# Means on 32-column tiles, a moved copy, and earlier zeroes in a four-layer graph network on one core

## The chip, the cores and the metric

The kernel runs on one core of a Trainium2 chip. The metric is the device time of one execution in microseconds (us), smaller is better. The core has five engines that work side by side and wait for each other by semaphores: TensorE (PE in the profile, its weight loads PEld), VectorE (DVE), ScalarE (ACT), GpSimd (POOL) and SyncE (SP). Transfers are issued from the queues of SP, ACT and POOL and share 16 DMA engines.

## The reference, cut to what matters

Four graph layers stand one behind the other, each as `x = x + layer(relu(layernorm(x)))`, on `x` of 8 batches, 2048 nodes, 64 features, all float32. The change touches layers 0 and 1 and the layer norm at the entrance of layer 2.

```python
def _layernorm(x):                       # over the 64 features
    m = mean(x); v = var(x)
    return (x - m) / sqrt(v + 1e-5)

def layer0(x, H, adj, W, W_ind, a_node, a_gn, a_ge, fcW, fcb, av):
    h = x @ W                                            # [8, 2048, 64]
    s = leaky_relu(h @ a_node, 0.2)
    alpha = softmax(where(H.T > 0, s, NEG))              # over the nodes of each of 64 hyperedges
    agg = einsum('ben,bnf->bef', alpha, h)
    beta = sigmoid((h @ a_gn)[:, None, :] + (agg @ a_ge)[:, :, None])
    all_he = elu(beta[..., None] * h[:, None] + (1 - beta[..., None]) * agg[:, :, None])
    deg = maximum(adj.sum(-1), 1.0)[:, None]
    industry = einsum('nm,bmf->bnf', adj / deg, x @ W_ind)
    attn = lambda f: tanh(f @ fcW + fcb) @ av
    coefs1 = softmax(where(H > 0, attn(elu(agg)), NEG))  # over the edges of each node
    g = einsum('bne,benf->bnf', coefs1, all_he)
    pair = stack([industry, g]); return sum(softmax(attn(pair)) * pair)

def layer1(x, adj, W, a):
    h = x @ W
    e = leaky_relu((h @ a[:64])[:, :, None] + (h @ a[64:])[:, None, :], 0.2)
    att = softmax(where(adj > 0.5, e, NEG_INF), axis=2)
    return elu(att @ h)

def layer2(x, adj, ...):   # three rounds of  v = relu([v, adj @ v] @ W1.T + b1) @ W2.T + b2
def layer3(x, adj, ...):   # x, adj @ x and (2 adj adj - 1) @ x, each through weights of the node's own
```

## The kernel before, in words

Two batches of 64 features fill the 128 partitions, so there are NP = 4 pairs p, each a 128 x 2048 matrix; CW = 512 columns are a chunk, NCW = 4 chunks make a pair, NT = 16 blocks of 128 nodes make 2048. The program goes through stages, which the trace shows one behind the other.

*Stage N* (to about 46 us) normalizes x and makes the first chunk of `industry`. *Stage E* (about 46 to 225 us) walks over the other three chunks in `industry(c)`: for each of eight loads `at` of the adjacency it issues 16 wide matmuls `acc` (L1098) and adds the load into the degree sum `ds`. Between them it pops small pieces of other work from the list `units`: `members(i)` (one for each block of nodes; it writes the high part `hi` and the rest `lo` of its features, stores both in DRAM, and adds to the sums `pg`, `pd` of the hyperedges), `listing` (which slots a node's edges take: `ranks`, `numbers`), and `table_1` to `table_5` (the tables by hyperedge). `hi` and `lo` come from a pool of three buffers each; their last 8 columns are set to zero by `begin()` (L1156) before each use. `table_5` makes 18 products `pn`, each of 8 columns. Stage E is not written in strict order: a scheduler at build time orders each engine's instructions, by priority and its own estimate of when operands come, and hands out buffers as they come free. An instruction issued through `InOrder` (or by `mm` and `turn` while `kit.strict` is set) stays behind everything that the source has issued before on its engine.

*Stage L* (about 225 to 375 us) goes over LT = 18 tiles of 114 nodes, NB = 3 blocks of slots in each: step j is block k = j % 3 of tile i = j // 3. TensorE's order is strict here. `features(i)` loads the `hi` and `lo` rows of a tile (`hhi`, `hlo`, three buffers each, 235 KB a load, POOL's queue), at step k = 2 for tile i + 2. `shares(i+1)`, also at k = 2, is the first reader of these (products `pm`). The slots of the first tile, `sT0` and `tmp0`, take one buffer of `hlo` and one of `hhi`. In the same steps the stage loads twelve 1 MB tiles `aT` of the adjacency (POOL's queue, `load_early`), and copies three pairs of x from DRAM to DRAM, 1 MB each (`x1_dram[i // 4]`, shown as `xd<-in_xT`). These copies are written at tiles 4, 8 and 12 and issued through `S = InOrder(nc.sync)`. `divided`, `back`, `done` scale a finished tile, turn it, and write it away.

*Stage O* (about 375 to 440 us) mixes `industry` and g, and `first_neighbours` makes layer 1's features of pair 0 in between.

*Stage A* (about 440 to 838 us) is layer 1's attention, four pairs in two halves of 16 blocks m. For each block, DVE makes two tiles `pt` (128 x 1024, L1793, six buffers), and TensorE multiplies them on tiles of 32 columns: `o` (features, weights `hS`) and `dn` (sums, weights `vd`). Between blocks, `between(m)` lets the next pair's preparation advance by `n` steps:

```python
n = (m in LATE) + 2 * (m == 2 * NT - 1) if last else (2, 0, 1, 0, 1)[m % 5] - (m % 20 == 0)
```

The preparation is `neighbour_steps(p + 1)`; per chunk it has a mean (`kit.norm_steps`: one matmul of 512 columns with the 128 x 128 matrix `avg` as weights), a variance (the same once more), and two steps `ph` with two maps each (weights of 128 columns, 132 columns moving). At the last pair it is `Layers23.front`, with four means and four variances by `norm_steps` at the blocks in LATE. The rows R that DVE needs (512 KB each, from `r_dram`) are loaded by SP's queue. For the last pair the pool `near` (R, and `l1_sb` with raw, sc, vd, wd, rstd, varn, rs, hS, xc, x, q, rr in this order) is closed, and two R buffers of a new pool `l1_late` take memory that partly was `l1_sb`'s. Pairs 0 and 2 have their `hS` in `l1_sb`, pairs 1 and 3 in `att_sb`.

*Layers 2 and 3* follow to the end.

Of the kernel before, what the change touches and what calls it, by code (L numbers as in the profile page):

```python
# [8 lines left out]
FP = mybir.dt.float32  # L9
# [7 lines left out]
P = 128  # L17
# [14 lines left out]
def cols(c, w=CW):  # L32
    return slice(c * w, (c + 1) * w)
# [603 lines left out]
class Kit:  # L637
# [110 lines left out]
    def use_ln_exp(self):  # L748
        self.tc.keep_in_program_order(self.nc.scalar.preload_act_table_set(LN_EXP))

    def norm_steps(self, dst, src, mean, var, xc, q):

        nc, mm = self.nc, self.mm
        n = dst.shape[-1] // CW
        for c in range(n):
            mm(mean[:, cols(c)], self.avg, src[:, cols(c)], start=True, stop=True)
        nc.vector.tensor_sub(xc, src, mean)
        nc.scalar.activation(q, xc, AF.Square)
        yield
        for c in range(n):  # L760
            if callable(var):
                var = var()
            mm(var[:, cols(c)], self.avg, q[:, cols(c)], start=True, stop=True)
        nc.scalar.activation(q, var, AF.Ln, bias=self.eps)
        nc.scalar.activation(q, q, AF.Exp, scale=-0.5)
        nc.vector.scalar_tensor_tensor(dst, xc, 0.0, q, op0=OP.max, op1=OP.mult)
        yield
# [6 lines left out]
def layer0(kit, hn, x1_dram, open_early, late_tile, between):  # L774
# [40 lines left out]
    def features(i):  # L815

        hi = lst.tile([P, B * F + 2 * B], FR, tag="hhi", name="hhi", bufs=3)
        lo = lst.tile([P, B * F + 2 * B], FR, tag="hlo", name="hlo", bufs=3)
        nc.gpsimd.dma_start(out=hi[0:LN], in_=hi_dram[of(i)].bitcast(FR))
        nc.gpsimd.dma_start(out=lo[0:LN], in_=lo_dram[of(i)].bitcast(FR))  # L820
        return hi, lo
# [16 lines left out]
    with ExitStack() as sA:  # L838
# [234 lines left out]
        with ExitStack() as s1:  # L1073
# [4 lines left out]
            pd = ps.tile([P, B], FP, tag="pd", name="pd")  # L1078
            units = []

            def industry(c, own):
# [62 lines left out]
            def members(i):  # L1144
# [4 lines left out]
                def begin():  # L1149
                    hi = sb.tile([P, BF_ + 2 * B], FR, tag="hi", name="hi", bufs=3)  # L1150
                    lo = sb.tile([P, BF_ + 2 * B], FR, tag="lo", name="lo", bufs=3)
                    es = sb.tile([P, B], FP, tag="es", name="es")
                    hs = sb.tile([P, B, F], FP, tag="hs", name="hs")
                    held.extend((hi, lo, es, hs))
                    for v in (hi, lo):
                        nc.vector.memset(v[:, BF_ + B :].bitcast(FP), 0.0)  # L1156
                    part(0)
# [93 lines left out]

            def table_5():

                pn = ps.tile([P, LT, B], FP, tag="pd", name="pn")
                for i in range(LT):
                    mm(pn[0:LN, i, :], MT[:, of(i)], kept["ea"][0:E, B : 2 * B], start=True, stop=True)
                nc.vector.tensor_scalar_max(rden[0:LN], pn[0:LN], 1e-30)
                nc.vector.reciprocal(rden[0:LN], rden[0:LN])
# [31 lines left out]
            units += rest  # L1290
            units += [last, table_1]
            units += [lambda: None, table_2, lambda: None, table_3, lambda: None, table_4, table_5, first_nodes]
            own = out_of(0, acc, None)
            for c in range(1, NCW):
                own = industry(c, own)
            for unit in own + units:
                unit()
        loaded = [features(i) for i in range(2)]

# [4 lines left out]
    with ExitStack() as s0:  # L1304
# [5 lines left out]

        V, A, G = InOrder(tc, nc.vector), InOrder(tc, nc.scalar), InOrder(tc, nc.gpsimd)
        mm = kit.mm
        flat = lambda a: a.rearrange("p b f -> p (b f)")
# [115 lines left out]
        for j in range(last + 2 * NB):  # L1429
            i, k = divmod(j, NB)  # L1430
            there = i + 1 < LT
            if k == 0:
                if 0 < i < LT:
                    shared(i)
                if 3 < i <= LT:
                    done(i - 4)
            if k == 2 and there:
                turned(i + 1)
            if j < last:
                pairs_of(j)  # L1440
            if k == 1 and i + 2 < LT:
                next_nodes(i + 2)
            if 1 <= j <= last:
                mixed(j - 1)
            if 3 <= j < last + 3:
                weighed(j - 3)
            if 5 <= j < last + 5:
                gathered(j - 5)
            if k == 0 and there:
                ranks(i + 1)  # L1450
            if k == 1 and there:
                turn(i + 1)
                edges(i + 1)
            if k == 2:
                if there:
                    shares(i + 1)
                if i + 2 < LT:
                    loaded.append(features(i + 2))
                if i < LT:
                    load_early(i)  # L1460
                if i in (4, 8, 12):
                    S.dma_start(out=x1_dram[i // 4], in_=t["xT"][i // 4])
                if 2 < i < LT:
                    back(i - 3)
                if 1 < i:
                    divided(i - 2)
                if i >= LT:
                    if i == LT:
                        back(i - 3)
                        done(i - 3)  # L1470
                    back(i - 2)
                    done(i - 2)
# [102 lines left out]
class Layer1:  # L1575
# [22 lines left out]
    def neighbour_steps(self, p):  # L1598
# [11 lines left out]
        for c in range(NCW):  # L1610
# [9 lines left out]
            if hS is None:  # L1620
                hS = (self.sb2 if p % 2 else sb).tile([P, NT, P], FP, tag="hS", name="hS", bufs=1)
            for g in range(2):
                if g:
                    yield
                ms = slice(4 * c + 2 * g, 4 * c + 2 * g + 2)
                ph = ps.tile([P, 2, P + 4], FP, tag="h", name="ph")
                for k in range(2):
                    j = 2 * g + k
                    mm(ph[:, k, :], hn[:, j * P : (j + 1) * P], Wx, start=True, stop=True)
                nc.scalar.activation(vd[:, ms, :], ph[:, :, P : P + 2], AF.Exp, scale=0.2)  # L1630
# [18 lines left out]
    def first_neighbours(self, xs, V, A):  # L1649
# [10 lines left out]
        rs = sb.tile([P, 2, NT], FP, tag="rs", name="rs", bufs=1)  # L1660
        hS = sb.tile([P, NT, P], FP, tag="hS", name="hS", bufs=1)
        mean, xc, q, out = {}, {}, {}, []
# [24 lines left out]

        def mapped():
            for m, ph in out:
                A.activation(hS[:, m : m + 2, :], ph[:, :, 0:P], AF.Copy)  # L1690
                V.tensor_copy(raw[:, m : m + 2, :], ph[:, :, P:])
            out.clear()
# [26 lines left out]
        def scaled(c):  # L1719
            h = hS[:, NC4 * c : NC4 * c + NC4, :].rearrange("p t (b f) -> p t b f", b=2)  # L1720
            V.tensor_tensor(
# [26 lines left out]
        self.first = [self.scores(0, 0, None) for b2 in range(2)]  # L1748
        self.now = hS, vd, wd
        at = lambda f, *a: lambda: f(*a)  # L1750
# [110 lines left out]
    def run(self, aT, following):  # L1861
# [10 lines left out]
        for p in range(NP):  # L1872
# [7 lines left out]
            def between(m):  # L1880
                if m % NT and ends:
                    ends.pop(0)()

                n = (m in LATE) + 2 * (m == 2 * NT - 1) if last else (2, 0, 1, 0, 1)[m % 5] - (m % 20 == 0)
                for _ in range(n):
# [494 lines left out]
```

## Time and profile before

| | us |
|---|---|
| runs of the kernel before | 1913.49 median of 3 (1909.81 to 1913.96) |
| the profiled execution | 1914.77 |
| its span | 1913.0 (mean granted TensorE clock 0.989) |
| TensorE busy | 1860.1 (97%) |
| DVE / ACT / POOL busy | 1176.0 / 464.2 / 314.9 |

The span runs from the first to the last instruction of the program; 1.8 us of the execution's own time lie around it. Instructions are named by engine, line and the tiles that they write and read; `L632` and `L737` are the helpers through which all ordered and all strict instructions go. A float32 matmul shows as two records. In brackets behind a line of the timeline stand the engine's idle time before it and what ended it.

### The profile page before, as it was taken

To read this page: it belongs to the slowest core of one execution; us is meant where nothing else is said; L and a number is where in the kernel's file an instruction comes from. 1 tells how busy PE (TensorE), PEld (TensorE's weight loads), DVE (VectorE), ACT (ScalarE), POOL (GpSimd) and SP (SyncE) were. 2 spreads that over 40 slices of the span, in tenths; PEclk is the share of its full clock that TensorE was granted. 3 is DMA by queue.
4 is the path that set the end of the run, shared out by engine and by line. 5 is a ranking of instruction groups with operands and counts; after the bars stand their busy time and mean duration, and the time that the engine had idled before them with its cause. 6 is when DMAs were issued, how large, how long until landed. Compare 5 with 4: busy or idle time off the path is not lost.

```text
span 1913.0 us, 25771 instructions
## 1 busy us (share of the span) xinstructions
PE 1860.1 (97%) x10172; PEld 1135.7 (59%) x10172; DVE 1176.0 (61%) x1869; ACT 464.2 (24%) x1048; POOL 314.9 (16%) x435
## 2 busy tenths in 40 slices
PE   7999989999999998999999999999999999999997
PEld 7877767543333232257775577765587755677653
DVE  7765579889898988953327642446623276523465
ACT  5422346573222120111210111310112201113000
POOL 4111278411000000000002110112200021101122
PEclk9999989999999999999999999999999999999999
DMA  7665386475222222213101021100122011121000
GB/s 205 169 198 176 126 227 169 108 176 117 57 56 57 56 49 53 62 42 100 61 12 30 26 61 56 50 23 19 33 66 61 23 25 31 45 72 50 5 20 13
DMA packets 86373, 142.60 MB, mean 75 GB/s; under 512 B 33800, under 2 KB 34056, under 8 KB 83568
## 3 DMA queue, kind: packets, MB, share of 16 engines
q1 hardware_dynamic: 65072, 83.78, 15.1%
q0 software_dynamic: 21040, 56.98, 12.3%
q8 instruction: 82, 1.34, 0.3%
q14 instruction: 51, 0.42, 0.1%
q10 hardware_dynamic: 128, 0.07, 0.0%
HBM read 106.85 MB, written 37.09 MB: 75 GB/s over the span
## 4 chain that ended last, share of the span: by engine, by line
PE 72%; issue 15%; DVE 5%; DMA 5%; POOL 2%; ACT 1%; SPq 0%; POOLq 0%; DVEq 0%; ACTq 0%
PE acc L737 32%; PE u L737 14%; PE o L737 5%; PE acc L1098 3%; PE py L737 3%; PE dn L737 3%; PE pgs L737 2%; PE pd L737 2%; DVE pt L1793 1%; PE var L737 1%; PE mean L737 1%; PE pv L737 1%; PE pm L737 1%; DMA hlo<-lo_dram 1%; DMA den<-d_dram 1%
## 5 line engine op out<-in xcount | busy, mean ns | idle before, releaser
L737 PE MATMUL acc<-aT,parts 128*128 128x512 f32 x1664 | 441.4, 409 | 0.0
L737 PEld LDWEIGHTS acc<-aT,parts 128*128 128x128 f32 x1664 | 306.6, 188 | 97.8 <-issue 39.2
L737 PE MATMUL o<-pt,hS 128*32 128x512 f32 x2048 | 237.9, 596 | 6.3 <-DVE pt L1793 5.2
L1793 DVE SCALAR_TENSOR_TENSOR pt<-R,wd,aT 128x1024 f32<-128x1024 f32 x188 | 230.7, 1279 | 21.0 <-DMA R<-r_dram 13.9
L737 PE MATMUL u<-W3f,y 64*128 64x512 f32 x1024 | 241.7, 589 | 0.0
L2255 DVE TENSOR_TENSOR pr<-u,embf 128x512 f32<-128x512 f32 x256 | 170.6, 687 | 109.7 <-PE u L737 102.7
L737 PEld LDWEIGHTS u<-W3f,y 64*128 64x128 f32 x1024 | 100.8, 187 | 119.0 <-issue 119.0
L737 PEld LDWEIGHTS o<-pt,hS 128*32 128x32 f32 x2048 | 64.8, 110 | 161.1 <-issue 144.4
L737 PE MATMUL u<-W3f,v 64*128 64x512 f32 x512 | 133.5, 596 | 0.0
L2267 POOL TENSOR_TENSOR fold<-fold 128x256 f32<-128x256 f32 x64 | 47.7, 745 | 496.1 <-DVE fold L2266 496.1
L737 PE MATMUL dn<-pt,vd 128*32 128x512 f32 x1024 | 125.0, 597 | 0.0
L2046 DVE TENSOR_TENSOR yb<-py,cb_f 128x512 f32<-128x512 f32 x32 | 22.1, 692 | 157.7 <-PE py L737 157.7
L1098 PE MATMUL acc<-at,Y 128*128 128x512 f32 x384 | 105.8, 418 | 0.2 <-ACT ev L1128 0.2
L737 PE MATMUL acc<-aTl,parts 128*128 128x512 f32 x384 | 99.7, 398 | 0.0
L2143 POOL TENSOR_TENSOR bq<-bq,xp 128x512 f32<-128x512 f32 x16 | 20.7, 1291 | 421.6 <-ACT xp L2126 421.6
L2259 DVE TENSOR_TENSOR pr<-pr 128x512 f32<-128x512 f32 x128 | 88.1, 688 | 2.2
L737 PEld LDWEIGHTS u<-W3f,v 64*128 64x128 f32 x512 | 56.6, 186 | 49.8 <-issue 36.5
L1793 DVE SCALAR_TENSOR_TENSOR pt<-R,wd,aTl 128x1024 f32<-128x1024 f32 x64 | 79.2, 1280 | 9.9 <-PE dn L737 6.2
L737 PEld LDWEIGHTS acc<-aTl,parts 128*128 128x128 f32 x384 | 71.5, 188 | 16.2
L1098 PEld LDWEIGHTS acc<-at,Y 128*128 128x128 f32 x384 | 71.4, 195 | 15.6 <-issue 1.8
L737 PEld LDWEIGHTS dn<-pt,vd 128*32 128x32 f32 x1024 | 31.0, 110 | 74.4 <-issue 69.9
L2060 DVE TENSOR_TENSOR parts<-tp,parts 128x512 fp32r<-128x512 f32 x16 | 11.1, 692 | 85.3 <-ACT parts L2059 85.3
(372 smaller groups left out, 2696.3 us busy)
## 6 DMA issues: line engine op xcount, KB each, us to landing
at<-in_adjT POOLq DMA_DIRECT2D x32, 512.0 KB, 5.2
raw<-in_adjT SPq DMA_DIRECT2D x64, 256.0 KB, 3.3
aT<-in_adjT POOLq DMA_DIRECT2D x12, 1024.0 KB, 7.9
xp<-xd SPq DMA_DIRECT2D x45, 256.0 KB, 2.9
R<-r_dram SPq DMA_DIRECT2D x14, 512.0 KB, 3.8
hlo<-lo_dram POOLq DMA_DIRECT2D x18, 235.1 KB, 3.7
hhi<-hi_dram POOLq DMA_DIRECT2D x18, 235.1 KB, 3.4
hi_dram<-hi SPq DMA_DIRECT2D x16, 264.0 KB, 3.2
```

The lines of the kernel that those rows point to most:

```text
L737: one = self.nc.tensor.matmul(*args, **kw)
L1098: mm(acc[p], Y[h][:, m, p, :], at[:, k, :], start=m + h == 0, stop=m == NT - 1 and h == 1)
L1793: V.scalar_tensor_tensor(pt, R, w, a.bitcast(FP), op0=OP.max, op1=OP.mult)
L2046: nc.vector.tensor_tensor(yb, py, bias[:, None, :].to_broadcast([P, 4, P]), op=OP.add)
L2060: nc.vector.tensor_tensor(lo, tp, hi.bitcast(FP), op=OP.subtract)
L2143: nc.gpsimd.tensor_add(bq, bq, xp)
L2255: nc.vector.tensor_tensor(a, u[h], emb[:, i, 8 * w : 8 * w + 8, None].to_broadcast([P, 8, F]), op=OP.mult)
L2259: nc.vector.tensor_add(pr[h], pr[h], a)
L2267: nc.gpsimd.tensor_add(fold[:, :, 0:2, :], fold[:, :, 0:2, :], fold[:, :, 2:4, :])
```

## The change

It has seven parts.

- `norm_steps` no longer multiplies by `avg` as one 128 x 128 tile. The new `averages` issues four matmuls, each with 32 columns of `avg` as weights, writing 32 partitions. `norm_steps` serves layer 1's chunks of pairs 1 to 3 and `front`.
- In `neighbour_steps` the four maps of a chunk are made in one step, into two PSUM tiles (tags `ln` and `h`), and `between` takes one step at m % 5 in (0, 2, 4). The maps keep their 128-column weights.
- In `first_neighbours`, `hS` is allocated at its first use in `mapped`, behind `xc`, `x` and `q`, no longer at the beginning.
- The three copies of x go through ACT's queue, in its program order.
- `members` takes its buffers from three pairs made once, whose zero columns are written once.
- `features(0)` and `features(1)` are issued in POOL's order among the last units of stage E; `table_5` is split into six units of three products, behind `first_nodes`.
- At the end of stage L, `back(14)`, `divided(15)` and `done(14)` move from tile 17 and step 54 to step 56.

```diff
+    def averages(self, dst, src):
+        for q in range(0, P, 32):
+            self.mm(dst[q : q + 32, :], self.avg[:, q : q + 32], src, start=True, stop=True, tile_position=(0, q))
...
-        for c in range(n):
-            mm(mean[:, cols(c)], self.avg, src[:, cols(c)], start=True, stop=True)
+        self.averages(mean, src)
...
-            mm(var[:, cols(c)], self.avg, q[:, cols(c)], start=True, stop=True)
+        self.averages(var, q)
...
-        nc.gpsimd.dma_start(out=hi[0:LN], in_=hi_dram[of(i)].bitcast(FR))
-        nc.gpsimd.dma_start(out=lo[0:LN], in_=lo_dram[of(i)].bitcast(FR))
+        queue = InOrder(tc, nc.gpsimd) if i < 2 else nc.gpsimd
+        queue.dma_start(out=hi[0:LN], in_=hi_dram[of(i)].bitcast(FR))
+        queue.dma_start(out=lo[0:LN], in_=lo_dram[of(i)].bitcast(FR))
...
+            his, loaded = [], []
+            for k in range(3):
+                his.append([sb.tile([P, BF_ + 2 * B], FR, name=f"{v}{k}", bufs=1) for v in ("hi", "lo")])
+                for v in his[k]:
+                    nc.vector.memset(v[:, BF_ + B :].bitcast(FP), 0.0)
...
-                    hi = sb.tile([P, BF_ + 2 * B], FR, tag="hi", name="hi", bufs=3)
-                    lo = sb.tile([P, BF_ + 2 * B], FR, tag="lo", name="lo", bufs=3)
+                    hi, lo = his[i % 3]
...
-                    for v in (hi, lo):
-                        nc.vector.memset(v[:, BF_ + B :].bitcast(FP), 0.0)
...
-            def table_5():
-                pn = ps.tile([P, LT, B], FP, tag="pd", name="pn")
-                for i in range(LT):
+            def table_5(part):
+                if part == 0:
+                    kept["pn"] = ps.tile([P, LT, B], FP, tag="pd", name="pn")
+                pn = kept["pn"]
+                for i in range(3 * part, 3 * part + 3):
                     mm(pn[0:LN, i, :], MT[:, of(i)], kept["ea"][0:E, B : 2 * B], start=True, stop=True)
+                if 3 * part + 3 < LT:
+                    return
...
-            units += [last, table_1]
-            units += [lambda: None, table_2, lambda: None, table_3, lambda: None, table_4, table_5, first_nodes]
+            units += [lambda: loaded.append(features(0)), last, lambda: loaded.append(features(1)), table_1]
+            units += [lambda: None, table_2, lambda: None, table_3, lambda: None, table_4, first_nodes]
+            units += [lambda k=k: table_5(k) for k in range(LT // 3)]
...
-        loaded = [features(i) for i in range(2)]
...
+        X = A
...
-                if 3 < i <= LT:
+                if 3 < i < LT:
                     done(i - 4)
...
+            if j == last + 2:
+                divided(LT - 3)
+                back(LT - 4)
...
+            if j == last + 2:
+                done(LT - 4)
...
-                    S.dma_start(out=x1_dram[i // 4], in_=t["xT"][i // 4])
-                if 2 < i < LT:
+                    X.dma_start(out=x1_dram[i // 4], in_=t["xT"][i // 4])
+                if 2 < i < LT - 1:
                     back(i - 3)
-                if 1 < i:
+                if 1 < i and i != LT - 1:
                     divided(i - 2)
...
-            for g in range(2):
-                if g:
-                    yield
+            phs = [ps.tile([P, 2, P + 4], FP, tag=k, name="ph") for k in ("ln", "h")]
+            for j in range(4):
+                mm(phs[j // 2][:, j % 2, :], hn[:, j * P : (j + 1) * P], Wx, start=True, stop=True)
+            for g, ph in enumerate(phs):
                 ms = slice(4 * c + 2 * g, 4 * c + 2 * g + 2)
-                ph = ps.tile([P, 2, P + 4], FP, tag="h", name="ph")
-                for k in range(2):
-                    j = 2 * g + k
-                    mm(ph[:, k, :], hn[:, j * P : (j + 1) * P], Wx, start=True, stop=True)
...
-        hS = sb.tile([P, NT, P], FP, tag="hS", name="hS", bufs=1)
...
         def mapped():
+            if self.now is None:
+                self.now = sb.tile([P, NT, P], FP, tag="hS", name="hS", bufs=1), vd, wd
+            hS = self.now[0]
...
-                n = (m in LATE) + 2 * (m == 2 * NT - 1) if last else (2, 0, 1, 0, 1)[m % 5] - (m % 20 == 0)
+                n = (m in LATE) + 2 * (m == 2 * NT - 1) if last else m % 5 in (0, 2, 4)
```

More of the change, by code (lines that the diff above doesn't have):

```diff
@@ L749, in use_ln_exp @@
         self.tc.keep_in_program_order(self.nc.scalar.preload_act_table_set(LN_EXP))
+    def averages(self, dst, src):
+        for q in range(0, P, 32):
+            self.mm(dst[q : q + 32, :], self.avg[:, q : q + 32], src, start=True, stop=True, tile_position=(0, q))
     def norm_steps(self, dst, src, mean, var, xc, q):
-        nc, mm = self.nc, self.mm
-        n = dst.shape[-1] // CW
-        for c in range(n):
-            mm(mean[:, cols(c)], self.avg, src[:, cols(c)], start=True, stop=True)
+        nc = self.nc
+        self.averages(mean, src)
         nc.vector.tensor_sub(xc, src, mean)
@@ L759, in norm_steps @@
         yield
-        for c in range(n):
-            if callable(var):
-                var = var()
-            mm(var[:, cols(c)], self.avg, q[:, cols(c)], start=True, stop=True)
+        if callable(var):
+            var = var()
+        self.averages(var, q)
         nc.scalar.activation(q, var, AF.Ln, bias=self.eps)
@@ L1719, in scaled @@
         def scaled(c):
-            h = hS[:, NC4 * c : NC4 * c + NC4, :].rearrange("p t (b f) -> p t b f", b=2)
+            h = self.now[0][:, NC4 * c : NC4 * c + NC4, :].rearrange("p t (b f) -> p t b f", b=2)
             V.tensor_tensor(
@@ L1748, in first_neighbours @@
         self.first = [self.scores(0, 0, None) for b2 in range(2)]
-        self.now = hS, vd, wd
+        self.now = None
         at = lambda f, *a: lambda: f(*a)
```

## Prediction

> **What bounds the kernel now.** I read the page first: parts 1 and 2.
>
> ```profile
> PE 1860.1 (97%) x10172; PEld 1135.7 (59%) x10172; DVE 1176.0 (61%) x1869; ACT 464.2 (24%) x1048; POOL 314.9 (16%) x435
> PEclk9999989999999999999999999999999999999999
> ```
>
> TensorE is busy for 97% of the span, so time can only go where it idles, runs at a reduced clock, or does needless work. PEclk dips in the slices of stages E and L. I asked the windows view for suspect stretches; after the stretch it gives busy time by engine, then the granted clock.
>
> ```profile
> 173.20:180.40 7.20, 7.20 (x28) 5.98 (x27) 3.39 (x8) 2.06 (x5) 1.26 (x2) 0.53 0.03 9
> 211.40:218.20 6.80, 6.80 (x19) 5.43 (x19) 4.89 (x5) 0.00 (x0) 0.00 (x0) 0.54 0.00 0
> 237.00:252.00 15.00, 6.78 (x18) 5.08 (x19) 6.87 (x10) 2.82 (x6) 7.99 (x11) 0.66 0.98 278
> 737.00:750.00 13.00, 7.83 (x55) 1.83 (x54) 8.43 (x7) 0.00 (x0) 1.73 (x3) 0.74 0.40 123
> ```
>
> In the first two TensorE is full and the clock is half; in the other two it idles for some 8 and 5 us, and the clock drops too. The timeline shows what went before each.
>
> ```profile
> 158.48 0.07 DVE L1156 MEMSET hi<- 128x8 f32 x1 [2.14 <-DMA hi_dram<-hi]
> 160.55 0.72 PE L1163 MATMUL ph<-W0x,hn 128*128 128x132 f32 x4 [1.47 <-DVE rank L918]
> 172.88 0.80 PE L1119 MATMUL deg<-ds,ones_r 128*128 128x512 f32 x2 [2.09 <-DVE ds L632]
> 207.70 4.16 PE L1256 MATMUL pn<-ea,MT 64*114 64x8 f32 x36
> 211.79 9.66 PE L1098 MATMUL acc<-at,Y 128*128 128x512 f32 x29
> 228.26 1.81 SPq L632 DMA_DIRECT2D xd<-in_xT  x3
> 231.62 0.56 POOL L820 DMA_DIRECT2D hlo<-lo_dram  x1
> 245.22 0.38 PE L737 MATMUL pm<-hlo,sT 114*128 114x16 f32 x1 [8.24 <-DMA hlo<-lo_dram]
> 714.93 22.41 SPq L1782 DMA_DIRECT2D R<-r_dram  x2
> 742.91 2.77 PE L737 MATMUL o<-pt,hS 128*32 128x512 f32 x10 [5.17 <-DVE pt L1793]
> ```
>
> A zeroing of 0.07 us holds DVE for 2.14 us until a store has landed; `rank` and later `ds` queue behind such zeroings, and TensorE waits for both. The narrow `pn` run for 4.16 us and leave the clock halved. The three copies, written for tiles 4, 8 and 12, are issued together at 228.26, just ahead of the `hlo` that TensorE then awaits for 8.24 us. Of the last pair's two R loads the second leaves SP 22 us after the first, when pair 2's last `o` is done.
>
> Stage A, last, by the timeline (start, length):
>
> ```profile
> 474.16 0.72 PE L737 MATMUL ph<-W1x,xc 128*128 128x132 f32 x4
> 474.81 3.64 PE L737 MATMUL o<-pt,hS 128*32 128x512 f32 x32
> 478.38 0.72 PE L737 MATMUL ph<-W1x,xc 128*128 128x132 f32 x4
> 478.93 1.02 PE L737 MATMUL mean<-x,avg_f 128*128 128x512 f32 x2
> 479.88 1.92 PE L737 MATMUL dn<-pt,vd 128*32 128x512 f32 x16
> 771.36 1.13 PE L737 MATMUL var<-v,avg_f 128*128 128x512 f32 x2
> 772.41 3.64 PE L737 MATMUL o<-pt,hS 128*32 128x512 f32 x32
> ```
>
> From start to start, `var` among 32-column work takes 1.05 us, one `ph` pair 0.65, `ph` with `mean` 1.50.
>
> **What the Trainium skill says.** *TensorE: Matmul & The Clock Gate*, Part 1: the clock is halved after an idle window of about 3.4 us. The trace agrees for idling, and shows more: 4.16 us of 8-column products did it too. *TensorEngine Tiling (Array Packing)*, Key Properties: changing the tiling mode drains the array; the 1.05 us against 0.86 us of streaming (16 records of `o` take 1.71 us, so 8 take 0.86) agree. *DMA: Bandwidth & Descriptors*, Issuing engines are not separate DMA queues: all queues run on the same 16 DMA engines, so ACT's queue isolates nothing; what can help is the moment of issue.
>
> **The change, part by part.**
>
> *Member buffers (E).* 32 zeroings of 65 ns become 6 at the stage's start, where three already wait 1.40 us for stage N; alone that is 2 us of DVE beside TensorE. What counts is the queueing: the gaps before 160.55 and 172.88 (1.5 and 2.1 us). The wait for the store does not vanish: ACT's copy into `hi` and DVE's `lo` now carry it, later, and behind them stand `es`, `hs` and the next member. The landing at 158.4 comes before the `hi` copy of 161, so mostly it has passed. With the second gap goes the half clock of 173 to 180: twelve narrow `pm` took 2.50 us there against 1.33 at 155; `acc`, `ph`, `pg` lose another 2.1; in all 3.3.
>
> *`table_5` split.* 28 steps of the 29 `acc` after `pn` take (9.66-0.40)/28 = 0.331 us, at full clock (3.83-0.40)/15 = 0.229: 2.8 us lost. Split, three products (0.7 us) lie between eight `acc` (1.85). In front of stage L's own narrow start they could still trip the clock, so 0 to 2.8. *Pinned `features(0)`, `(1)`*: a `hhi` load held POOL's queue for 7.2 us at 154 to 161 with an `at` behind it; that frees POOL, but no `acc` waited for it: nothing. Their landing, at 165 so far, may move to 200 and is needed at 226. Stage E is not in strict order, so everything may shift. Sum of E 1.5+2.1+3.3+2.8 = 9.7; I take 7.5 (2 to 10).
>
> *Copies through ACT.* The three landed 6.0, 9.0 and 12.0 us after issue; `aT` and `hlo`, issued at 231.02 and 231.62, landed together 3.4 to 3.7 us after the last of them. With nothing in the way an `aT` lands in 5.1 us, so both by about 236.5, and the product is due at 236.6. TensorE saves 8.6 us start to start, and the slow stretch behind: `pm` 1.88 for 0.9, `pd`, `pa`, `pgs` likewise, 3.2 in all. Together 11.8. What is late next: each copy now sits at steps 14, 26 and 38, between the `hhi` and `hlo` of a tile. A copy takes the DMA engines for about 3.5 us (the spacing of the landings). A `hlo` has about 2.0 us to spare (issued 263.45, landed 266.92, due 268.96): up to 1.5 us stall each, below the clock's window. ACT pays 3 x 0.58 us for issuing, queued ahead of `ex`, with 28 of 47 us busy: hidden behind TensorE. SP loses nothing that waits. 11.8 - 0.3 - 2 = 9.5 (5 to 12).
>
> *Stage L's end.* `divided(15)` (0.6 us of DVE) leaves the queue ahead of the last `mix`; but the third-last `pgs` now needs it for its PSUM buffer. 0.5 (-1 to 1.5).
>
> *`hS` moved.* In the memory map of the compiled kernel before, `hS` of pair 2 lies at bytes 81,376 to 89,567 of a partition, the second R of `l1_late` at 79,744 to 83,839: it waits for pair 2's last read. Behind `xc`, `x`, `q` (8192 bytes), `hS` begins at 89,568, and R meets raw to rs and `xc`, all read by the preparation's end. Then R leaves at about 715. `xp` of `front` overlaps the new `hS`, but is issued at 737 today and due at block 4. From pair 2's last `o` (16 records of the group at 734.99, to 736.70) to the mean at 756.96 lie 80 records of `o` and 32 of `dn`, 112 x 0.107 = 12.0 us; 20.3 passed. I take 8 (7 to 8.5).
>
> *32-column means.* Four products of 8 records in all take 0.86 us if they run like `o`. `var` costs 1.05 plus 0.11 (a `dn` before it 1.83 instead of 1.72) plus 0.03: 1.19. Saved 0.33; times 8 for `front`: 2.6. A chunk before: 1.19 + (0.65+0.14) + (1.50+0.14) = 3.62; after: 0.86 + 0.86 + 4 maps in one step (0.65+0.14+0.44) = 2.95. Twelve chunks: 8.0. The maps keep 128-column tiles, so the words of the change promise too much there. ACT's twelve small reads of `ph` (about 2.8 us) end before the next mean needs `ln` (2.6 us on, first half 1.4). DVE makes a block's `pt` in 2 x 1.21 = 2.42 us (seven in 8.46) against TensorE's 24 records x 0.107 = 2.57: 87 us a pair with everything, TensorE after 94; still TensorE. 10 of 10.6 (5 to 11).
>
> Sum 7.5+9.5+0.5+8+10 = 35.5: from the profiled 1914.8 (span 1913.0 and 1.8 around it) to 1879.3; the median stands 1.3 lower, so **1878**.
>
> **Rivals.**
> *The stalls move.* The copies stall three tiles beyond 3.4 us with the clock after them, and stage E reshuffles: L gives 3, E 2: 1913.5-23.5 = 1890. For it: a copy starved `hlo` by 10 us. Against: that took three copies.
> *DVE becomes the bound in stage A.* It has 2.42 against 2.57 us and six buffers; the means give 5 and R 5, the others hold: 1886. Against: in 512 to 535 TensorE never waits.
> *Slower: four means one after the other.* `o` shows two products sharing one moving tile side by side, never four. Were they serial, a group costs 4 x 0.86 = 3.4 us; 32 groups lose 2.57 each, 82 us, against 25.5 from the rest and 2 from the maps: about 1968. It decides from a group of 0.86 + 28/32 = 1.7 us on.
> *The change doesn't do what it says*: the scheduler hands out the same buffers and order, only the copies, `hS` and means count: 1886.
>
> **How the numbers follow.** The forecast 0.62; moved stalls 0.16; DVE 0.08; no effect of the E parts 0.08; serial 0.04; reshuffling that cancels everything 0.02. A measurement of this kernel can tell about 0.2% (3.8 us) from no change. Faster 0.94, same 0.02, slower 0.04. The best ends sum to 43 (1870); the weak cases reach 1890, with their spread 1895. Range 1868 to 1895.
>
> **What would show it.** Right: `pm<-hlo` without a long wait near 230; `mean` and `var` with form 128*32, about 0.86 us a group; both R issued near 715 (minus the earlier gains); no half clock behind `pn`. Wrong: `pm` waiting for `hlo` at tiles 6, 10 and 14; mean groups above 1.7 us; DVE named as releaser of `o`; memset waits reappearing as `lo` or `hi` waits with TensorE behind.

## The result and the profile after

| | us |
|---|---|
| runs of the changed kernel | 1880.54 median of 4 (1880.27 to 1882.07) |
| runs of the kernel before, on the same chip | 1913.72 median of 4 (1909.81 to 1917.74) |
| ratio | 0.9828, 95% interval 0.9807 to 0.9849 |
| span of the profiled execution | 1878.1 (before: 1913.0); mean granted clock 0.996 (before: 0.989) |

By the medians the change saves 33 us, where 35.5 had been forecast (1878 us; 1880.5 were measured). In the two profiled executions the spans differ by 34.9 us. Where these lie is read from the times at which TensorE starts a few fixed products; stage N, and layers 2 and 3, are alike in the two profiles within 0.4 us.

| stretch, bounded by | before | after | gain | forecast |
|---|---|---|---|---|
| N and E, to the last `acc<-at,Y` | 225.18 | 214.66 | 10.5 | 7.5 |
| junction and L, to the last `pm<-hlo` | 357.26 | 337.55 | 9.2 | 9.5 |
| end of L and O, to the first `o` | 440.56 | 423.06 | -2.2 | 0.5 |
| A, to the last `o` | 838.48 | 803.95 | 17.0 | 18 |
| rest | | | 0.4 | 0 |

The sum of the profile is right within 1 us, and in part by luck, because two errors of some 3 us cancel: stage E gained more than forecast, and the end of stage L lost.

The page of the changed kernel, parts 1 and 2:

```profile
PE 1840.7 (98%) x10364; PEld 1146.9 (61%) x10364; DVE 1174.5 (63%) x1843; ACT 463.1 (25%) x1048; POOL 311.7 (17%) x435
PEclk9999999999999999999999999999999999999999
```

No slice shows a dip any more. TensorE issues 192 records more (the means in four tiles) and is still busy 19 us less. Four stretches of the windows view follow (busy us by engine, then the granted clock). The second and the fourth are the places where the kernel before stood idle for `hlo` and for R:

```profile
217.50:221.00 3.50, 3.50 (x11) 2.64 (x9) 2.20 (x4) 1.96 (x5) 2.31 (x2) 0.51 0.39 131
226.00:241.00 15.00, 15.00 (x67) 10.09 (x65) 14.37 (x24) 7.27 (x16) 12.51 (x16) 1.00 0.86 261
350.50:356.00 5.50, 5.09 (x14) 2.67 (x14) 0.86 (x2) 2.08 (x8) 0.00 (x0) 0.69 0.01 3
701.00:714.00 13.00, 13.00 (x128) 3.98 (x124) 12.51 (x11) 1.32 (x2) 0.62 (x1) 1.00 0.14 42
```

In 226 to 241, where tile 2 once waited for its `hlo`, and in 701 to 714, where pair 3 once waited for its R, TensorE is full at full clock. Two stretches at a reduced clock are left: at the start of stage L and at its end. The second has a new cause, and the timeline shows it, together with the new places of the copies and of R (start, length; in brackets the idle time before and what ended it):

```profile
205.10 1.36 PE L1263 MATMUL pn<-ea,MT 64*114 64x8 f32 x12
249.72 0.58 ACTq L632 DMA_DIRECT2D xd<-in_xT  x1
350.91 2.02 PE L737 MATMUL pgs<-mix,S 128*114 128x512 f32 x2 [3.37 <-DVE gn L632]
684.97 0.80 SPq L1796 DMA_DIRECT2D R<-r_dram  x2
719.09 1.22 DVE L1865 TENSOR_TENSOR res<-o,den 128x1024 f32<-128x1024 f32 x1 [3.41 <-DMA den<-d_dram]
```

The copies leave one by one (the others at 279.45 and 308.71). Both R leave within 0.8 us of each other. Two waits are new: `pgs` waits 3.37 us for the quotient `gn` of tile 15, and DVE waits 3.41 us for `den`, because pair 3 now runs ahead of it. A chunk of stage A by the timeline:

```profile
443.40 1.04 PE L737 MATMUL mean<-x,avg_f 128*32 128x512 f32 x8
444.26 3.62 PE L737 MATMUL o<-pt,hS 128*32 128x512 f32 x32
455.54 1.17 PE L737 MATMUL ph<-W1x,xc 128*128 128x132 f32 x8
456.63 3.64 PE L737 MATMUL o<-pt,hS 128*32 128x512 f32 x32
```

From start to start a group of four means takes 0.86 us (444.26 - 443.40), and the four maps in one step 1.09.

### The profile page after: what moved, and what is told of

It is laid out like the page before. It is cut to its first block, busy times and chain, and to the rows that moved or that the text cites. A ratio compares the mean times of both kernels' runs of the same rounds, so it can differ in the third digit from the quotient of the medians.

```text
span 1878.1 us, 26150 instructions
## 1 busy us (share of the span) xinstructions
PE 1840.7 (98%) x10364; PEld 1146.9 (61%) x10364; DVE 1174.5 (63%) x1843; ACT 463.1 (25%) x1048; POOL 311.7 (17%) x435
## 4 chain that ended last, share of the span: by engine, by line
PE 50%; issue 10%; DMA 2%; POOL 2%; DVE 1%; POOLq 0%; ACT 0%; SPq 0%; DVEq 0%
PE acc L737 31%; PE u L737 14%; PE py L737 2%; PE pv L737 1%; POOL fold L2281 1%; PE var L737 1%; PE mean L737 1%; DMA xd<-e 0%; DMA W3f<-in_L_gnn_weight 0%; DMA den<-d_dram 0%; PE tx L744 0%; POOL ot L2282 0%; PE tv L744 0%; PE tp L744 0%; DVE pt L1807 0%
## 5 line engine op out<-in xcount | busy, mean ns | idle before, releaser
L737 PE MATMUL o<-pt,hS 128*32 128x512 f32 x2048 | 247.1, 593 | 2.0 <-DVE pt L632 1.2
L737 PEld LDWEIGHTS o<-pt,hS 128*32 128x32 f32 x2048 | 79.1, 110 | 143.8 <-issue 112.8
L737 PE MATMUL dn<-pt,vd 128*32 128x512 f32 x1024 | 134.9, 593 | 0.0
L1106 PE MATMUL acc<-at,Y 128*128 128x512 f32 x384 | 101.7, 405 | 0.3 <-ACT ev L1136 0.2
L737 PEld LDWEIGHTS dn<-pt,vd 128*32 128x32 f32 x1024 | 40.7, 110 | 67.7 <-issue 49.2
L2074 DVE TENSOR_TENSOR parts<-tp,parts 128x512 fp32r<-128x512 f32 x16 | 11.1, 692 | 85.3 <-ACT parts L2073 85.3
```

What stands on the lines that cost most here:

```text
L737: one = self.nc.tensor.matmul(*args, **kw)
L1106: mm(acc[p], Y[h][:, m, p, :], at[:, k, :], start=m + h == 0, stop=m == NT - 1 and h == 1)
L2074: nc.vector.tensor_tensor(lo, tp, hi.bitcast(FP), op=OP.subtract)
```

## The experiments

The first six undo one part of the change. A caution comes first, since it decides how their times are read.

### The scatter of stage N

Several variants' profiles lag behind the changed kernel's by 1.3 to 3.3 us before they reach any edit. So the changed kernel was run once more as it stands.

> The changed kernel once more, as it stands, for its time beside the variants and for the stretch at 15 to 27 us in stage N, which the change does not touch: there the second and third py run of 8 products takes 1.16 us in some profiles and 2.08 in others. Theory: that stretch differs from one execution to the next, by 0 to 3 us, whatever the kernel: the time stays at 1880.5 within 1.5 us, and this profile may show either. Rival: it belongs to the variants (the changed kernel always comes out of it early): then 1.16 us again, and the variants' medians carry up to 3 us that are not of their edits.

Measured: 1881.62 us (1879.79 to 1882.79, 5 runs), ratio to before 0.9831 (0.9817 to 0.9844). The second run of eight `py`, in the timeline of the first profile of the changed kernel and then of this one:

```profile
20.24 1.16 PE L737 MATMUL py<-W_indf,hn 128*128 128x128 f32 x8
```

```profile
20.20 2.08 PE L737 MATMUL py<-W_indf,hn 128*128 128x128 f32 x8
```

The same kernel, the same products, nearly twice the time: the theory holds. TensorE's first products take nearly twice as long as later ones of the same form, and this ends a few us earlier or later in one execution than in another: the next `py` run, at 23.49, took 1.16 us here, and 2.07 or 2.08 in other profiles. (The windows view gives the clock as 1.00 all through these us, so the slow rate is seen in the durations alone.) Hence each effect below is read between two products around its own place, and stage N's lag is taken off; a median can carry up to 3 us of it. This profile differs in a second way: the half clock at the start of stage L, 217.5 to 221 in the other, isn't there, and from the last `acc` to the third `pd<-ntab`, at 221.68 in the first profile and so behind that stretch, it needed 6.0 us for 7.0. So the half clock at the junction was worth 1.0 us, and whether it comes differs between executions of one kernel.

### The copies on SP's queue

```
-        X = A
+        X = S
```

> The changed kernel with one line undone: the three copies of x1 go through SP's queue again. Theory: what mattered is the moment of issue. On SP the three leave together near 218, ahead of the hlo of tile 6; TensorE waits some 8 us in one pm and works at half clock behind it; the time rises by about 11.5 us, to 1892. Rival: after the other edits SP is no longer held up there (the loads for the first tiles are now issued in order on POOL), so the copies leave in their places on either queue; then the time rises by less than 2 us, to at most 1882.5.

Measured: 1887.33 us (4 runs; ratio to before 0.9866, 0.984 to 0.9893). Between the first `pd<-ntab` and the last `pm<-hlo` of stage L 6.5 us were lost, and nothing elsewhere. Its timeline and its view of waits (us in total, times, longest):

```profile
217.87 1.81 SPq L632 DMA_DIRECT2D xd<-in_xT  x3
```

```profile
PE pm L737 <- DMA hlo<-lo_dram: 5.3, 1, 5.3
```

The burst of three is back, and so is the one wait of `pm`; the rival is out. The `hlo` that is awaited is that of tile 2, here and in the kernel before (the recorded text calls it tile 6): the wait stands ahead of the seventh `pm<-hlo`, and each tile has three. The wait is 5.3 us for the 8.24 of before: here the first copy leaves 9.2 us ahead of the start of that `pm` run, before it was 8.2 us (236.50 - 228.26), and the `hlo` landed 15.0 us after the first copy, then 16.9. What a burst costs depends on where it falls.

Between the sixth and the ninth `pd<-ntab`, around tile 2, the changed kernel's lead over the kernel before grows by 11.5 us (from 9.5 to 21.0), and its lead over this variant by 7.9 (from 0.1 to 8.0). So 7.9 us of the 11.5 are the copies'; the other 3.6 go with the new place of the burst, by subtraction and not by a run of their own. Behind tile 2 the changed kernel gives 1.3 us back: from the first `pm<-hlo` of tile 3 to that of tile 17 it takes 102.7 us, the kernel before 101.4 and this variant 101.3, with TensorE busy all the time. That leaves 6.5. The edit changes the queue and the moment of issue together; copies on SP's queue in the places of tiles 4, 8 and 12 were not tried.

### Zeroing at each use

```
-                    hi, lo = his[i % 3]
+                    hi = sb.tile(..., tag="hi", name="hi", bufs=3)
+                    lo = sb.tile(..., tag="lo", name="lo", bufs=3)
...
+                    for v in (hi, lo):
+                        nc.vector.memset(v[:, BF_ + B :].bitcast(FP), 0.0)
```

> The changed kernel with one part undone: the member buffers come from a pool of three again and are zeroed at each use (32 zeroings on DVE). Theory: the zeroings hold DVE until a store has landed, rank and ds are late behind them, TensorE idles twice for some 3.6 us in all and runs at half clock behind the second: plus 5 to 7 us, to about 1886.5. Rival: stage E's 10 us come from the split pn and from the loads that no longer hold POOL's queue; then undoing the zeroing costs less than 2 us, at most 1882.5.

Measured: 1893.20 us (4 runs; ratio 0.9894, 0.9868 to 0.9921). Of the 12.3 us by which its last `acc` is late, 3.1 are stage N's; 9.1 are the zeroing's. Its timeline, and one of its windows:

```profile
171.86 0.15 DVE L1172 SCALAR_TENSOR_TENSOR lo<-ph,hi 128x4 fp32r<-128x4 f32 x1 [4.92 <-issue]
175.00 1.22 DVE L632 TENSOR_TENSOR ds<-ds,at 128x1024 fp32r<-128x1024 f32 x1
176.36 1.19 PE L1123 MATMUL deg<-ds,ones_r 128*128 128x512 f32 x2 [4.68 <-DVE ds L632]
```

```profile
172.00:183.50 11.50, 7.14 (x26) 6.02 (x27) 5.55 (x18) 2.50 (x7) 0.73 (x1) 0.57 0.13 50
```

DVE stands for 4.92 us. The view names nothing that ended this, but the trace has it: the store `hi_dram<-hi`, issued at 164.34, landed at 171.82, and the zeroing of `hi`, which waits for that store, ran at 171.88, right beside the `lo` shown. So `ds` is late, `deg` and with it TensorE waits 4.68 us, and from about 174 to 184 the clock is halved. The theory's chain is there, but in place of two waits with 3.6 us in sum there is one of 4.7; 8.3 us are lost around it, 9.1 in all, not 5 to 7. The rival is out.

### `table_5` in one unit

```
-            units += [lambda k=k: table_5(k) for k in range(LT // 3)]
+            units += [lambda: [table_5(k) for k in range(LT // 3)]]
```

> The changed kernel with the 18 products of table_5 in one unit again. Theory: the run of 4 us of 8-column products halves the clock for the 29 acc behind it, as before: plus 2.8 us there, minus up to 0.9 us, since the half clock at the start of stage L that stands in the changed kernel may fall away: plus 1.9 to 2.8 us, about 1883. Rival: with the zeroing waits gone the clock no longer falls behind pn (it had been halved once just before, at 173 to 180): within 0.7 us of the changed kernel.

Measured: 1883.16 us (4 runs; ratio 0.9834, 0.9817 to 0.985). In the profile, stage N apart, stage E ends 0.7 us later, the junction gives 0.5 back, and stage L loses 1.6 up to its last `pm`. The windows of this kernel behind `pn`:

```profile
208.10:212.10 4.00, 4.00 (x12) 3.14 (x12) 3.66 (x4) 0.00 (x0) 0.00 (x0) 0.57 0.00 0
```

Behind the 3.76 us of 8-column products the clock is halved, with no wait near; behind the same products in four pieces it is not (1.00 from 198 to 213 in the changed kernel). That mechanism is shown. It lasts 4 us, though, where it lasted over 6 in the kernel before, and the four pieces together take 4.2 us for the 3.8 of the whole, so the net in stage E is 0.7 us where up to 2.8 had been priced. The 1.6 us in stage L (waits of `px` for POOL and ACT of 0.6 us each, a half clock at 222 to 225) were not foreseen by either side.

### The first two tiles' loads at the end of stage E

```
-        queue = InOrder(tc, nc.gpsimd) if i < 2 else nc.gpsimd
+        queue = nc.gpsimd
...
-            units += [lambda: loaded.append(features(0)), last, lambda: loaded.append(features(1)), table_1]
+            units += [last, table_1]
...
+        loaded = [features(i) for i in range(2)]
```

> The changed kernel with the loads of the first two tiles at the end of stage E again and not held in order on POOL's queue. Theory: no acc waited for POOL's queue, so nothing: within 0.5 us in stage E (stage N's own scatter aside) and 1880 to 1883. Rival: a hhi load that waits for its store holds POOL's queue for 7 us, an at behind it comes late and acc waits: plus 1 to 3 us in stage E.

Measured: 1887.25 us (4 runs; ratio 0.986, 0.9837 to 0.9883). Stage N cost 3.3 us of this; up to the last `acc` the edit cost nothing (-0.1), as the theory says, and no `acc` waited for POOL. But from there to the first `pd<-ntab` 2.9 us went. Its timeline:

```profile
216.74 0.62 PE L1127 MATMUL deg<-ds,ones_r 128*128 128x512 f32 x2
220.28 0.41 PE L737 MATMUL px<-sT,Q 114*128 114x384 f32 x1 [2.00 <-DVE ev L1140]
```

Stage E isn't in strict order, and the last column's `deg` now comes at 216.74, four `acc` records before the end; in the changed kernel it comes at 209.13, sixteen before the end (4.3 us earlier, stage N's lag taken off). DVE and ACT work on `rdeg` and `ev` behind it, and stage L's first `px` waits 2.0 us. Both theories missed: the loads cost no wait of their own, their place changes the order that the scheduler makes of everything else. That part was priced at nothing and is worth some 3 us: the wait of 2.0 us, and a reduced clock behind it (0.76 in 220 to 223).

### The means as one 128 x 128 product

```
-        for q in range(0, P, 32):
-            self.mm(dst[q : q + 32, :], self.avg[:, q : q + 32], src, ..., tile_position=(0, q))
+        self.mm(dst, self.avg, src, start=True, stop=True)
```

> The changed kernel with each mean and variance of layer 1 as one 128x128 product again, the steps and the four maps in one step left as changed. Theory: each of the 32 groups costs 0.33 us more (1.19 for 0.86), so plus 10.6 us: 1891. Rival: the gain of stage A lies in the merged steps (fewer places where maps stand among the 32-column products), and the form of the means is worth little: plus 0 to 3 us, at most 1883.5.

Measured: 1891.03 us (4 runs; ratio 0.9888, 0.9861 to 0.9914). From the first `o` to the last it takes 10.7 us more than the changed kernel; the rest is unchanged. The timeline of this kernel:

```profile
448.73 1.13 PE L737 MATMUL var<-q,avg_f 128*128 128x512 f32 x2
449.78 3.64 PE L737 MATMUL o<-pt,hS 128*32 128x512 f32 x32
```

1.05 us from start to start for 0.86, with the steps and maps as changed. 10.7 us over 32 groups is 0.33 each: 0.19 in the group itself, the rest beside it (a `dn` run ahead of such a product takes 1.85 us from start to start for 1.73). So the form of the product is the gain. The first three pairs hold 24 of the groups and lose 7.4 us here; of the 8.8 us that they won between the two kernels, some 1.4 are left for the merged steps, by subtraction.

### `hS` of the first pair allocated first

```
+        hS = sb.tile([P, NT, P], FP, tag="hS", name="hS", bufs=1)
         mean, xc, q, out = {}, {}, {}, []
...
-        self.now = None
+        self.now = hS, vd, wd
```

> The changed kernel with hS of the first pair allocated first again, as before. Theory: the second R of the last pair shares bytes with pair 2's hS, leaves SP only after pair 2's last o, and TensorE waits at the start of pair 3 and runs at half clock for a time: plus 8 us there; the wait of 1.3 us for den in the same pair falls away or stays behind it, so plus 6 to 8 us: about 1887. Rival: the R moved forward because the shorter stage A gives the queue other neighbours, not because of the bytes: plus less than 1 us.

Measured: 1887.24 us (4 runs; ratio 0.9867, 0.9835 to 0.9899), 2.1 us of its profile being stage N's; stage A takes 6.6 us more. Its timeline:

```profile
687.04 26.02 SPq L1794 DMA_DIRECT2D R<-r_dram  x2
718.91 2.77 PE L737 MATMUL o<-pt,hS 128*32 128x512 f32 x10 [5.44 <-DVE pt L1805]
```

The second R leaves 26 us after the first, `pt` waits for it, TensorE for `pt` (5.44 us), and the clock falls behind that (0.76 in 713 to 727). Where the buffer lies decides it; the queue's neighbours do not. At the start of pair 3 7.9 us are lost; 1.3 of them come back a few blocks on, because the late pair does not meet the wait of 3.41 us for `den`, which is missing here.

### The end of stage L: three arrangements

First the order of before:

```
-            if j == last + 2:
-                divided(LT - 3)
-                back(LT - 4)
...
-                if 1 < i and i != LT - 1:
+                if 1 < i:
                     divided(i - 2)
```

> The changed kernel with the end of stage L as it was before the change: divided(15) in its place at step 53, back and done of the last tiles likewise. Theory: the reordering made divided(15) stand on DVE behind the last weighed; the third-last pgs, which needs its PSUM buffer, waited 3.37 us for it, and the clock was halved behind the wait. Without it the wait of pgs for gn is gone and the stretch from the last pairs to the last pgs is 2.3 us shorter (about 15.6 us where it now is 17.9): the time falls by some 2.3 us, to 1878. Rival: the 2.3 us are not of the order but of the faster steps before (DVE, the same as ever, is now the later one at the end of the stage); then the time stays within 0.7 us.

Measured: 1882.85 us (4 runs; ratio 0.9834, 0.9817 to 0.985). The wait of `pgs` for `gn` is gone, and yet nothing is won: from the last `pm<-hlo` to the first `o` of stage A it takes 86.9 us, the changed kernel 85.5 and 86.7 in its two profiles, the kernel before 83.3. Its timeline:

```profile
353.60 3.62 PE L737 MATMUL pgs<-mix,S 128*114 128x512 f32 x4
```

Those four take 1.88 us in the kernel before and in the changed one: here the clock is half for 8.5 us (0.50 in 352.5 to 361), behind three short waits of TensorE (0.85, 1.79 and 1.06 us). The theory's number fell. The rival's held (within 0.7 us of the changed kernel, once the 1.9 us of stage N in this profile are taken off), and what it says of DVE's work is left to the next run. How long a half clock lasts is not a safe reading, either: in the first profile of the changed kernel the windows view gives 0.50 for 351 to 354 and full clock behind it, in the second 0.50 for 351 to 357, with the same wait ahead. Then `divided(15)` alone, moved two steps forward:

```
             if j == last + 2:
-                divided(LT - 3)
                 back(LT - 4)
+            if j == last:
+                divided(LT - 3)
```

> The changed kernel with divided(15) alone moved: issued at step 54, behind mixed(53) and ahead of the last two weighed, while back and done of the last tiles stay as changed. Theory (PSUM buffer behind DVE's order): gn is ready before POOL's last product, pgs starts some 2.5 us earlier and the half clock behind it doesn't come: 3 to 5 us less than the changed kernel, about 1876.5. Rival (DVE's whole work at the end of the stage decides, whatever its order): the last pgs still ends with DVE's last product, and the time stays within 0.7 us of the changed kernel.

Measured: 1879.88 us (4 runs; ratio 0.9822, 0.9806 to 0.9839); the stretch takes 82.9 us, 2.6 less than the changed kernel's first profile, and the clock is 1.00 throughout. The medians alone, 1879.88 and 1880.54, do not tell the two kernels apart. The stretch does: it takes 82.9, 82.9 and 81.0 us in the three profiles with `divided(15)` early, and 85.3 to 86.7 in the nine with the changed kernel's order. So the place of `divided(15)` on DVE's queue is the cause of the 3.37 us, and DVE's total work isn't. One long wait was left in this profile's timeline:

```profile
351.52 0.58 PE L744 MATMUL ptg<-ident_f,gn 114*128 114x114 f32 x4 [1.79 <-DVE gn L632]
```

These transposes of tile 16 stand ahead of the last two `pgs` on TensorE. The last kernel below puts them behind.

### `end` one block later, and the best version

```
-        return [lambda: None, lambda: None, end]
+        return [lambda: None] * 3 + [end]
```

> The changed kernel with one more empty step ahead of end in attend, so that a half's quotient is formed one block later. Theory: in the changed kernel DVE waits 3.4 us for den at 719 in the first half of pair 3, no pt is made meanwhile, and TensorE waits 1.3 us in o; with one block more (2.6 us or longer) den has landed: minus 1.3 us, about 1879. Rival: the six pt buffers leave DVE so close to TensorE in that half that its 0.7 us of product, wherever it stands, makes TensorE wait as long: within 0.4 us.

Measured: 1881.17 us (4 runs; ratio 0.9827, 0.9807 to 0.9848), with 2.8 us of stage N in its profile. Stage A is 1.3 us shorter. Its timeline, to be read beside the 3.41 us of the changed kernel:

```profile
723.35 1.23 DVE L1865 TENSOR_TENSOR res<-o,den 128x1024 f32<-128x1024 f32 x1 [1.18 <-DMA den<-d_dram]
```

DVE still waits, but no longer than its lead over TensorE lasts, and no `o` of that half waits; in the changed kernel one waited 0.7 us, and the rest of the 1.3 is not resolved. As the theory says, in the profile; the median, with stage N's lag in it, does not show it. Both repairs together:

> The changed kernel with both repairs: divided(15) issued at step 54 ahead of the last two weighed, and end one block later. Theory: the two lie in different stages and add, 2.2 us and 1.3 us by the profiles: about 1877. Rival: TensorE, relieved in one place, meets a wait or a half clock elsewhere; then no less than 1879.

Measured: 1877.69 us (1876.64 to 1879.14, 5 runs; ratio 0.981, 0.979 to 0.9829), 1.5 us of its profile being stage N's. The end of stage L takes 82.9 us again, stage A 1.2 us less: they add. And with tile 16's transposes behind the last `pgs`:

```
                     if i == LT:
                         back(i - 3)
                         done(i - 3)
-                    back(i - 2)
-                    done(i - 2)
+                    else:
+                        for n in (i - 3, i - 2):
+                            back(n)
+                            done(n)
```

> As the kernel with both repairs, and back(16) (transposes that wait 1.8 us for gn, with the last pgs queued behind them on TensorE) issued behind the last pgs. Theory: the last pgs ends some 1.5 us earlier, and of the end of stage L about 1 us is saved beside the kernel with both repairs: about 1876. Rival: stage O begins by waiting for the last gn, its transposes and ACT's copies anyway; then within 0.5 us of the kernel with both repairs.

Measured: **1874.87 us** (1872.24 to 1876.97, 5 runs), ratio to before 0.9791 (0.9771 to 0.9811); the stretch takes 81.0 us, 1.9 less, about twice what was expected. Every one of its five runs lies below every one of the changed kernel's nine (1879.79 at the lowest). The timeline of its last `pgs`:

```profile
353.90 1.11 PE L737 MATMUL pgs<-mix,S 128*114 128x512 f32 x2 [0.21 <-DVE mix L632]
```

## Why the prediction was right, and which terms were not

*Member buffers, the split and the loads: 7.5 forecast, 10.5 measured, of which 0.3 are stage N's.* Both waits went and with them both half clocks; the full sum of 9.7 was there, and the deduction for a reshuffled order was not needed. Read in place, the changed kernel's lead grows by 8.0 us up to the `acc` at 172.64 (180.96 before), where 6.9 had been priced for the zeroing, and by 2.2 from there to the last `acc`, where `pn` lies (up to 2.8). Undone one by one, the parts give other sizes. Zeroing costs 9.1 us. `table_5` costs 0.7 in stage E: its half clock had been priced at the length that it had beside other troubles. The loads, priced at "nothing" because no `acc` waited for POOL, cost 2.9. These are 12.7 us, more than the whole gain: the losses do not add, since each undone part makes an order of its own.

*Copies: 9.5 forecast, 9.2 measured over the junction and stage L.* The mechanism and its 11.8 were right: 11.5 us were gained at tile 2. From these go 1.0 us ahead of it, at the junction, where the second profile of the changed kernel lost nothing, and the 1.3 behind it. Neither is the loss that the forecast had taken off, a new stall of up to 1.5 us at each of three tiles, 2 us in all: TensorE has no wait for a DMA in stage L of the changed kernel. So the net figure is near by luck, and the step that failed is the slack. The forecast gave a `hlo` 2.0 us to spare because it paired the load issued at 263.45, which landed at 266.92, with the product of the tile before, at 268.96. The timeline of the kernel before has the load, the seventh of 18, and the first product that reads it, that of tile 6, the seventh tile (each product waits for its own load's semaphore):

```profile
263.45 0.54 POOL L820 DMA_DIRECT2D hlo<-lo_dram  x1
276.66 0.26 PE L737 MATMUL pm<-hlo,sT 114*128 114x16 f32 x1
```

That load had 9.7 us to spare. Paired in this way, the loads of tiles 3 to 17 had 7.2 to 11.2 us in the kernel before. They have 2.5 to 10.7 in the changed kernel: less, but enough. The `hlo` issued behind the first two copies took 6.9 us each to land, and still landed 4.5 and 4.9 us before their products (259.04 for 263.56, 287.96 for 292.89).

*Stage L's end: a gain of 0.5 forecast, 2.2 lost.* The working saw the right thing (the third-last `pgs` needs `divided(15)` for its PSUM buffer) and priced DVE's 0.6 us only. The price is the place: behind the last `weighed` in DVE's queue, 3.37 us of TensorE, with the clock after it. Moving that one instruction gives it back (82.9 for 85.5). Why the order of before spent only some 3 us at half clock in the kernel before, and 8.5 in the variant with all the other parts changed, is open: the waits ahead of it are alike (0.72 and 1.79 there, 0.85, 1.79 and 1.06 here), no run here varied them one at a time, and two executions of the changed kernel differ by 3 us there as well.

*`hS` and the means: 18 forecast, 17.0 measured.* A group takes 0.86 us as worked out, 10.7 us in all by the undone form against 10.6 by the forecast's 0.33 a group. `hS` undone costs 6.6, below the forecast's 7 to 8.5. R leaves at 685, 30 us before the 715 of the forecast, and 26 of these are gains made before pair 3 (17.5 up to stage A and 8.8 in its first three pairs). What is missing there, and in the sum, is about the wait for `den`, on which the forecast had nothing: 1.3 us, which `end` one block later gave back.

Of the rivals, four serial means would have shown 3.4 us a group; 0.86 stands there. DVE never became the bound: `o` waits for `pt` 1.9 us in all, 1.2 of them at the stage's first block, where the kernel before waited as long. Moved stalls did come, in two other places than the rival had them (`gn` and `den`), together 3.5 us (2.2 and 1.3).

## What to carry to other kernels

Price an instruction in a queue by what stands behind it, not by its length: zeroings of 0.07 us, a product of 0.69 us and three copies cost 9.1, 2.6 and 6.5 us here, and all three were cured by another place. Before a slack is read off, pair each load with the product that waits for it: the pair one tile too early made 2.0 us of 9.7. After a change that removes waits, read the new profile for the wait that is next: two edits of a few lines gave 1.3 and 2.6 us, a third 1.9. And where a scheduler orders part of the work, "no wait" is not "no effect": pinning a load shifted an unrelated `deg` and with it 2.9 us.

## What the hardware showed that was not expected

The clock falls without a long wait. 3.76 us of 8-column products did it with TensorE busy throughout (0.57 in the next 4 us), and it fell to 0.50 for 8.5 us behind waits of 0.85, 1.79 and 1.06 us with work between them. The Trainium skill, *TensorE: Matmul & The Clock Gate*, Part 1, names an idle window of about 3.4 us; the 3.37 us before `pgs` fit it, these two do not. Its other sentence, that the clock follows how busy the array has been lately, is wide enough for all three. These runs give no rule that would forecast it: in the run with `divided(15)` early, waits of 0.85, 0.48 and 1.79 us left the clock at 1.00, and at the start of stage L one execution of the changed kernel fell to 0.51 and another did not. The same part puts the scatter of the first transition to full clock, under sustained work, at half a us; here, where TensorE still waits now and then, it moved by 1.3 us between two executions of one kernel and by up to 3.3 between kernels alike up to there.

Four products of 32 columns each that share one moving operand run side by side: 0.86 us for all four, where one product of 128 columns put among such work takes 1.05.
